# Two attention layers on one core: a score bank emptied and refilled by 256 columns instead of 512

## Chip, core and metric

The kernel is one program on one core of a Trainium2 chip. It is written in Python on a framework that gives each engine its own queue of instructions, worked off in order, and sets the semaphore waits from what the instructions read and write. The metric is the device time of one execution in microseconds (us), taken as the median of several runs. A profiled execution has its own time and a span, which runs from the start of its first to the end of its last instruction.

Five engines appear: PE (TensorE, matmuls; its weight loads are listed apart as PEld), DVE (VectorE), ACT (ScalarE), POOL (GpSimd) and SP (SyncE, which issues DMAs).

## The reference

Four blocks, each an attention-like layer and a feed-forward layer, are added to x of shape 4 x 1024 x 128 (batch, tokens, features), all in float32. The change touches only the two softmax attentions, in blocks L2 and L3. Both get layer-normed x, and `run` adds their output to x.

```python
# L2: 8 heads of 16
scores = einsum('bhsd,bhtd->bhst', q, k) / sqrt(16)
p = softmax(scores, axis=-1)
att = einsum('bhst,bhtd->bhsd', p, v)
out = att.reshape(S, B, D, H).sum(axis=-1).reshape(B, S, D)

# L3: 16 heads of 8, keys in blocks of 64, over which this is scanned
scores = einsum('bhqd,bhkd->bhqk', Q, K_blk) / sqrt(8)
m_new = maximum(m, scores.max(-1, keepdims=True))
corr, exp_scores = exp(m - m_new), exp(scores - m_new)
chunk_sum = exp_scores.sum(-1, keepdims=True)
l = chunk_sum * corr + chunk_sum            # not l * corr
out = out * corr + einsum('bhqk,bhkd->bhqd', exp_scores, V_blk)
# after the last block: out / l, then out @ out_w.T + out_b
```

## The kernel before

**Layout.** `attention` serves both layers. Heads go in groups of four. Head j of a group lies on partitions 32j to 32j+31, so that four matmuls of 32 rows can run beside each other in four row strips of TensorE. L2 has 8 groups (4 batches, 2 each) and L3 has 16. Queries and keys are kept transposed (features on partitions, 1024 tokens along the row). One further row holds minus the row maximum in q and ones in k, so a score comes out with its maximum already subtracted. The values have a column of ones, which makes the sums of the softmax come out beside the output.

**Turns and rounds.** A group is worked on twice, 16 turns each time. First it is *scanned*: query blocks of 128 against 512 keys at a time, only to find the row maxima. Then it is *weighed*: 128 keys (`kc`) against 512 queries (`n`) at a time, exponentials taken and multiplied with the values. While group m is weighed, group m + 1 is scanned. A turn has two rounds. A round, in the order of the code of the loop at the end of `attention`, is:

1. `weigh` of a first head: one matmul of 128 x 512 into a PSUM bank `pb` (line 1319), then its exponential by ACT into `es` (line 1323).
2. `score` of two heads of the other group into a two-bank tile `pa` (line 1265), and a maximum over it by DVE (line 1273 or 1277).
3. `weigh` of a second head, with another bank `pb` and another exponential.
4. `gather` (line 1341): the exponentials of an earlier turn times the values of four heads, 256 query columns, into the bank `po`.
5. Jobs that belong to this turn and round, such as projections, `negate` (maxima into q by way of DRAM) and `collect`.

In round 0 of a turn the weighed heads are 2 and 3 and the scored ones 0 and 1; in round 1 it is the other way round. So each round's four matmuls lie in four different row strips. A float32 matmul appears in the profile as two passes, each with a weight load of its own. `gather` is skipped in the round that would take the first half of a `kc` of 0, and takes all 512 columns one round later.

**Counts.** There are (8 + 16) x 16 x 2 = 768 weighing rounds, 24 x 16 x 4 = 1536 exponentials, and 3072 passes at line 1319. In the first 16 turns of a layer nothing is weighed (`scan_alone`), and in the last 16 nothing is scanned.

**Banks.** PSUM has eight banks of 512 float32 per partition. Here `pa` takes four (two tiles of two), `po` one, and a pool called `sm` has three, which rotate: each `weigh` takes the next. Call a round's first head A and its second head B. With two banks taken per round and three in rotation, B of a round takes the bank that A of the round before has left, and A takes the bank that B of two rounds before has left. An engine's queue is in order: when the weight load of B waits for its bank, the `gather` behind it waits too.

**Elsewhere, for comparison.** Block L0 has other PSUM tiles that the prediction reads. `wide` (line 324) is four banks: one use writes the columns 0 to 255 of each bank (inputs `bt`, `kt`), and ACT copies them to `kk` (line 348); the other use writes columns 256 to 511 (inputs `qp`, `kt`), and DVE multiplies them with a mask into `mt` (line 413). `tp` is one bank of two halves, which ACT copies one after the other into `kt` (line 339) and `bt` (line 341). Line 486 has four matmul passes of 256 columns behind each other.

Of the kernel before, what the change touches and what calls it, by code (L numbers as in the profile page):

```python
# [9 lines left out]
F32 = mybir.dt.float32  # L10
AF = mybir.ActivationFunctionType
ALU = mybir.AluOpType
AX = mybir.AxisListType
PSUM = bass.MemoryType.PSUM

P = 128
# [11 lines left out]
class Net:  # L28
# [1087 lines left out]
    def attention(self, H, HD, scale, weights, prepare, finish, last=False):  # L1116
# [13 lines left out]
        nc, tc = self.nc, self.tc  # L1130
# [3 lines left out]
        TURNS = 2 * TPB  # L1134
        NBM = 9 if last else 2
        wq, wk, wv = weights
        with ExitStack() as c:
# [1 line left out]
            two = c.enter_context(tc.tile_pool(name="at2", bufs=2))  # L1139
            dram = c.enter_context(tc.tile_pool(name="atd", bufs=1, space=bass.MemoryType.DRAM))  # L1140
            pap = c.enter_context(tc.tile_pool(name="ata", bufs=2, space=PSUM))
            sm = c.enter_context(tc.tile_pool(name="ats", bufs=3, space=PSUM))
            pop = c.enter_context(tc.tile_pool(name="ato", bufs=1, space=PSUM))
            qcol, kcol, vrow = prepare(one, sm)
            md = dram.tile([M, 2, 4, 4, P], F32, tag="md", name="md")
            ones = one.tile([1, 4, 32], F32, tag="ones1", name="ones1")
            nc.gpsimd.memset(ones, 0.0)
            nc.gpsimd.memset(ones[:, :, HD : HD + 1], 1.0)
            cp = sm.tile([P, 1], F32, tag="sm", name="cp")
            nc.tensor.matmul(  # L1150
                cp, lhsT=ones.rearrange("p a b -> p (a b)"), rhs=self.ones[0:1, 0:1], start=True, stop=True
            )
            col = one.tile([P, 1], F32, tag="onec", name="onec")
            nc.vector.tensor_copy(col, cp)
            kring = [one.tile([P, SEQ], F32, tag=f"k{i}", name=f"k{i}") for i in range(3)]
            qring = [one.tile([P, SEQ], F32, tag=f"q{i}", name=f"q{i}") for i in range(3)]
            zero = one.tile([4, 256], F32, tag="zero", name="zero")
# [123 lines left out]
            def scan_alone(m, turn):  # L1281


                st = state[m]
                i, n = turn // 2, turn % 2
                if n == 0:
                    both = [scan(m, turn, hp) for hp in range(2)]
                    for j in range(4):
                        both[j // 2][0](j)
                    for _, reduce in both:  # L1290
                        reduce()
                    return
                banks = [sm.tile([P, 512], F32, tag="sm", name="pb") for _ in range(3)]
                banks.append(pop.tile([P, 512], F32, tag="po", name="pb"))
                for j in range(4):
                    r = slice(32 * j, 32 * j + 32)
                    nc.tensor.matmul(
                        banks[j], lhsT=st["q"][r, i * P : (i + 1) * P],
                        rhs=st["k"][r, n * 512 : (n + 1) * 512], start=True, stop=True,
                    )  # L1300
                for j in range(4):
                    out = st["bm"][i // 4][:, i % 4, j, :]
                    if last:
                        nc.vector.tensor_reduce(  # L1304
                            out[:, 1:9], banks[j].rearrange("p (c s) -> p c s", c=8), axis=AX.X, op=ALU.max
                        )
                    else:
                        nc.vector.tensor_reduce(out[:, n : n + 1], banks[j], axis=AX.X, op=ALU.max)  # L1308

            def weigh(m, turn, j):  # L1310

                st = state[m]
                n, kc = turn // TPB, turn % TPB
                es = st.setdefault("es", {})
                if turn not in es:
                    es[turn] = two.tile([P, 4, 512], F32, tag="es", name="es", bufs=5)
                pb = sm.tile([P, 512], F32, tag="sm", name="pb")
                r = slice(32 * j, 32 * j + 32)
                nc.tensor.matmul(  # L1319
                    pb, lhsT=st["k"][r, kc * P : (kc + 1) * P], rhs=st["q"][r, n * 512 : (n + 1) * 512],  # L1320
                    start=True, stop=True,
                )
                nc.scalar.activation(es[turn][:, j, :], pb, AF.Exp, scale=scale)  # L1323

            def gather(m, turn, half):

# [44 lines left out]
            for b in range(NB):  # L1371

                t = b * G * TURNS
# [5 lines left out]
            for m in range(M):  # L1379
                t = m * TURNS  # L1380
# [15 lines left out]
            t = 0  # L1396
            while t < (M + 1) * TURNS or jobs:
                scans, weighs = TURNS <= t < M * TURNS, TURNS <= t < (M + 1) * TURNS
                if t < TURNS:
                    scan_alone(0, t)  # L1400
                for rnd in range(2):

                    other = 2 - 2 * rnd
                    if scans:
                        score, reduce = scan(t // TURNS, t % TURNS, rnd)
                    if weighs:
                        weigh(t // TURNS - 1, t % TURNS, other)
                    if scans:
                        for j in range(2):
                            score(2 * rnd + j)  # L1410
                        reduce()
                    if weighs:
                        weigh(t // TURNS - 1, t % TURNS, other + 1)

                    w, half = (t - 2, 1) if rnd == 0 else (t - 1, 0)
                    if TURNS <= w < (M + 1) * TURNS:
                        gather(w // TURNS - 1, w % TURNS, half)
                    for what, args in jobs.pop((t, rnd), ()):
                        what(*args)
                t += 1  # L1420
# [10 lines left out]
    def l2_attn(self):  # L1431
        nc, a = self.nc, self.a2
        H, HD = 8, 16
        self.layernorm(twice=(a["gamma"], a["beta"]))
        with self.tc.tile_pool(name="a2", bufs=1) as one:

            wv = one.tile([P, P], F32, tag="wvs", name="wvs")
            nc.vector.tensor_reduce(wv, a["wv"].rearrange("p (d j) -> p d j", j=8), axis=AX.X, op=ALU.add)

            def prepare(pool, psum):  # L1440
                row = pool.tile([1, P], F32, tag="row", name="row")
                nc.vector.tensor_reduce(row, a["bv"].rearrange("p (d j) -> p d j", j=8), axis=AX.X, op=ALU.add)
                vp = psum.tile([P, P], F32, tag="sm", name="vp")
                nc.tensor.matmul(vp, lhsT=self.ones[0:1, :], rhs=row, start=True, stop=True)
                vrow = pool.tile([P, P], F32, tag="vrow", name="vrow")
                nc.vector.tensor_copy(vrow, vp)
                return a["bq"], a["bk"], vrow

            def finish(b, o, sums, corr, pool, pair):

                rec = pool.tile([P, 8, H], F32, tag="rec", name="rec")

                def weights():
                    tp = pair("tp").rearrange("p (r h) -> p r h", r=8)
                    sv = sums.rearrange("p (s r) -> p r s", r=8)
                    for r in range(8):
                        nc.tensor.transpose(tp[:, r, 0:H], sv[:, r, :], self.ident[0:H, 0:H])
                    nc.vector.reciprocal(rec, tp[:, :, 0:H])

                def turn():  # L1460
                    tp = pair("tp2").rearrange("p (r h d) -> p r h d", r=8, h=H)
                    ov = o.rearrange("p (s r) -> p r s", r=8)
                    for r in range(8):
                        nc.tensor.transpose(tp[:, r, :, :].rearrange("p h d -> p (h d)"), ov[:, r, :], self.ident)
                    ob = pool.tile([P, H, 8, HD], F32, tag="ob", name="ob")
                    nc.vector.tensor_mul(
                        ob.rearrange("p h r d -> p r h d"), tp, rec.unsqueeze(3).to_broadcast([P, 8, H, HD])
                    )
                    xs = self.x[:, b * TPB : (b + 1) * TPB, :]
                    nc.gpsimd.tensor_add(xs, xs, ob.rearrange("p h r d -> p h (r d)"))  # L1470

                return [weights, turn]

            self.attention(H, HD, 0.25, (a["wq"], a["wk"], wv), prepare, finish)

    def l2_ffn_load(self):
# [349 lines left out]
```

## Time and profile before

| what | value |
|---|---|
| median of 3 runs | 2668.34 us (2666.43 to 2669.78) |
| the profiled execution | 2665.29 us |
| its span, first to last instruction | 2663.6 us |
| PE busy | 2417.5 us, 91% of the span |
| DVE, ACT, POOL busy | 1795.2, 1501.7, 293.0 us |
| stretch with weighing in L2 (1012 to 1480 us) | 468 us: PE 467.6, ACT 284.2 busy |
| stretch with weighing in L3 (1607 to 2530 us) | 923 us: PE 921.7, ACT 574.0 busy |
| granted TensorE clock in both stretches | 1.00 |

The time of the profiled execution is 1.7 us above its span and 3.05 us below the median of the runs. The busy times count an engine as busy when any of its instructions runs. Four matmuls in four row strips are one busy stretch of PE, also when three of the strips have ended and the fourth is late.

### The profile page before, as it was taken

How to read it: one execution, taken by the hardware profiler on the slowest of the kernel's cores; microseconds unless marked ns; L12 is line 12 of the kernel's file. 1: busy time of each engine (PE TensorE's matmuls, PEld its weight loads, DVE VectorE, ACT ScalarE, POOL GpSimd, SP SyncE). 2: the span in 40 equal slices, each digit the busy share in tenths (PEclk: the TensorE clock that was granted, in tenths of full speed). 3: DMA queues.
4: the chain of work that ended last, by engine and by line, in shares of the span. 5: the costliest groups of instructions: out<-in, count | busy, mean ns of one | idle time of the engine just before them, and what ended most of it. 6: DMA issues, size and time to landing. Idle time of an engine off the chain costs nothing.

```text
span 2663.6 us, 51041 instructions
## 1 busy us (share of the span) xinstructions
PE 2417.5 (91%) x19913; PEld 1222.1 (46%) x19913; DVE 1795.2 (67%) x3670; ACT 1501.7 (56%) x3333; POOL 293.0 (11%) x525
## 2 busy tenths in 40 slices
PE   5687758899997979999999779999999999999968
PEld 3455535699995333333333443333333333333356
DVE  5888877476764767776774357767767776777233
ACT  4466468455554434665566635666666566666632
POOL 6012021000002530000000440000000000000011
PEclk8699879899997989999999879999999999999969
DMA  1333320000000001001000000000000000000000
GB/s 45 74 77 74 73 74 1 1 1 1 1 1 2 1 9 18 14 15 18 14 14 6 5 5 10 9 10 8 8 9 12 8 9 10 8 8 8 3 18 18
DMA packets 116719, 46.66 MB, mean 18 GB/s; under 512 B 88473, under 2 KB 111097, under 8 KB 116474
## 3 DMA queue, kind: packets, MB, share of 16 engines
q1 hardware_dynamic: 116474, 43.35, 8.2%
q8 instruction: 159, 2.61, 0.4%
q14 instruction: 86, 0.70, 0.1%
HBM read 17.04 MB, written 12.98 MB: 11 GB/s over the span
## 4 chain that ended last, share of the span: by engine, by line
PE 57%; DVE 4%; ACT 1%; POOL 1%; issue 1%; SPq 0%; DMA 0%; POOLq 0%; DVEq 0%; ACTq 0%
PE pb L1319 32%; PE po L1341 16%; PE pa L1265 2%; DVE bm L1277 1%; PE pp L1205 1%; PE pv L1186 1%; DVE bm L1304 1%; PE tp L158 1%; PE gp L1014 1%; PE rp L1743 1%; DVE bm L1308 0%; PE pr L1598 0%; PE rp L1520 0%; PE ph L1756 0%; POOL sg L1753 0%
## 5 line engine op out<-in xcount | busy, mean ns | idle before, releaser
L1323 ACT ACTIVATE es<-pb 128x512 f32<-128x512 f32 x1536 | 836.3, 594 | 536.1 <-PE pb L1319 381.8
L1319 PE MATMUL pb<-q,k 32*128 32x512 f32 x3072 | 956.5, 641 | 3.9 <-DVE bm L1308 1.7
L1265 PE MATMUL pa<-k,q 32*128 32x512 f32 x2944 | 846.0, 650 | 10.4 <-DMA q<-q 10.3
L1277 DVE TENSOR_REDUCE bm<-pa 128x2 f32<-128x1024 f32 x496 | 605.0, 1225 | 261.1 <-PE pb L1319 168.0
L1341 PE MATMUL po<-es,v 128*32 128x256 f32 (+1 forms) x5760 | 480.0, 405 | 0.0
L1319 PEld LDWEIGHTS pb<-q,k 32*128 32x128 f32 x3072 | 313.5, 183 | 350.7 <-ACT es L1323 189.8
L1341 PEld LDWEIGHTS po<-es,v 128*32 128x32 f32 x5760 | 114.2, 108 | 543.1 <-issue 508.2
L1273 DVE TENSOR_REDUCE bm<-pa 128x16 f32<-128x1024 f32 x240 | 293.2, 1222 | 97.3 <-PE pb L1319 60.7
L1265 PEld LDWEIGHTS pa<-k,q 32*128 32x128 f32 x2944 | 234.4, 186 | 37.0 <-issue 18.6
L152 POOL TENSOR_SCALAR xn<-x,rs,nm 128x128 f32<-128x128 f32 x112 | 50.3, 464 | 1204.6 <-DVE nm L125 1026.9
L366 DVE TENSOR_TENSOR pr<-T,L 128x31 f32<-128x31 f32 (+15 forms) x248 | 92.0, 371 | 28.0 <-DMA L<-ld 20.7
L369 DVE TENSOR_TENSOR T<-T,pr 128x31 f32<-128x31 f32 (+15 forms) x248 | 93.1, 375 | 8.5
L1348 DVE COPY oT<-po 128x512 f32<-128x512 f32 x48 | 32.8, 682 | 95.6 <-PE po L1341 95.6
L158 PE MATMUL tp<-ident,xn 128*128 128x128 f32 x224 | 47.0, 361 | 42.7 <-ACT xn L154 38.1
L821 ACT ACTIVATE w<-tr,half 128x128 f32<-128x128 f32 x128 | 47.1, 368 | 48.3 <-PE tr L819 45.6
L796 ACT ACTIVATE a<-hp,wb 128x128 f32<-128x128 f32 x128 | 47.1, 368 | 41.6 <-PE hp L792 40.1
L1081 PE MATMUL ep<-L_ffn_expert_w,xnT 128*128 128x512 f32 x128 | 66.8, 654 | 3.3 <-DVE x L1090 3.1
L324 PE MATMUL wide<-bt,kt 32*128 32x128 f32 x512 | 29.9, 360 | 43.9 <-DVE mt L413 31.7
L486 PE MATMUL sp<-ux,kn 128*128 128x256 f32 x128 | 46.1, 493 | 17.7 <-ACT ux L475 17.7
L158 PEld LDWEIGHTS tp<-ident,xn 128*128 128x128 f32 x224 | 33.9, 179 | 61.2 <-ACT xn L154 47.0
L804 DVE TENSOR_TENSOR dlt<-gr,mask 128x128 f32<-128x128 f32 x96 | 28.0, 292 | 48.3 <-PE gr L802 48.3
L853 ACT COPY dr<-tr 128x128 f32<-128x128 f32 x128 | 34.1, 266 | 43.1 <-PE tr L851 41.1
(466 smaller groups left out, 3598.8 us busy)
## 6 DMA issues: line engine op xcount, KB each, us to landing
ld<-kk SPq DMA_DIRECT2D x128, 32.0 KB
L<-ld SPq DMA_DIRECT2D x8, 512.0 KB
td<-T SPq DMA_DIRECT2D x8, 512.0 KB
tb<-td SPq DMA_DIRECT2D x128, 32.0 KB
md<-nt SPq DMA_DIRECT2D x192, 2.0 KB
q<-md SPq DMA_DIRECT2D x192, 2.0 KB
x<-in_L_attn_x_dram SPq DMA_DIRECT2D x4, 512.0 KB
od<-o SPq DMA_DIRECT2D x32, 64.0 KB
```

The source lines that it names most:

```text
L152: nc.gpsimd.tensor_scalar(xn[:, i, :], src[:, i, :], sl, bl, ALU.mult, ALU.add)
L158: nc.tensor.transpose(tp[:, i, :], xn[:, 4 * n + i, :], self.ident)
L366: nc.vector.tensor_mul(pv, T[:, 0 : j + 1, j : j + 1].to_broadcast(sh), L[:, j : j + 1, j + 1 :].to_broadcast(sh))
L369: nc.vector.tensor_sub(T[:, 0 : j + 1, j + 1 :], T[:, 0 : j + 1, j + 1 :], pv)
L796: nc.scalar.activation(self.a, self.hp, AF.Silu, bias=B1)
L1081: nc.tensor.matmul(ep.rearrange("p a b -> p (a b)"), lhsT=self.tok(t), rhs=ew[:, 4 * h : 4 * h + 4, :].rearrange("p a b -> p (a b)"), star ...
L1265: nc.tensor.matmul(pa[:, j % 2, :], lhsT=st["q"][r, i * P : (i + 1) * P], rhs=st["k"][r, n * 512 : (n + 1) * 512], start=True, stop=True,)
L1273: nc.vector.tensor_reduce(out[:, :, 1:9], pa.rearrange("p j (c s) -> p j c s", c=8), axis=AX.X, op=ALU.max)
L1277: nc.vector.tensor_reduce(out[:, :, n : n + 1], pa, axis=AX.X, op=ALU.max)
L1319: nc.tensor.matmul(pb, lhsT=st["k"][r, kc * P : (kc + 1) * P], rhs=st["q"][r, n * 512 : (n + 1) * 512], start=True, stop=True,)
L1323: nc.scalar.activation(es[turn][:, j, :], pb, AF.Exp, scale=scale)
L1341: nc.tensor.matmul(po[r, cols], lhsT=vring[b % 2][:, kc, 4 * g + j, :], rhs=es[:, j, cols], start=kc == 0, stop=True, skip_group_check=True,)
```

## The change

- The pool `sm` gets one buffer per tag, and three tiles `eb` with the tags sm0, sm1 and sm2 are made once. `weigh` takes them in turn, by a counter, where it took the pool's next tile before. `scan_alone` uses the same three. So the rotation of banks stays as it was.
- The first head of a round (`early`) is still one matmul over 512 columns, but its exponential is taken by two ACT instructions of 256 columns each.
- The second head is two matmuls of 256 columns each into its bank, and its exponential is one ACT instruction of 512 columns as before.
- Two small tiles, `cp` and `vp`, which are used once before the rounds, get a tag of the new pool.

```diff
-            sm = c.enter_context(tc.tile_pool(name="ats", bufs=3, space=PSUM))
+            sm = c.enter_context(tc.tile_pool(name="ats", bufs=1, space=PSUM))
...
+            eb = [sm.tile([P, 512], F32, tag=f"sm{i}", name=f"eb{i}") for i in range(3)]
...
-                banks = [sm.tile([P, 512], F32, tag="sm", name="pb") for _ in range(3)]
+                banks = list(eb)
...
-            def weigh(m, turn, j):
+            turned = [0]
+
+            def weigh(m, turn, j, early):
...
-                pb = sm.tile([P, 512], F32, tag="sm", name="pb")
+                pb = eb[turned[0] % 3]
+                turned[0] += 1
                 r = slice(32 * j, 32 * j + 32)
-                nc.tensor.matmul(
-                    pb, lhsT=st["k"][r, kc * P : (kc + 1) * P], rhs=st["q"][r, n * 512 : (n + 1) * 512],
-                    start=True, stop=True,
-                )
-                nc.scalar.activation(es[turn][:, j, :], pb, AF.Exp, scale=scale)
+                whole, halves = (slice(0, 512),), (slice(0, 256), slice(256, 512))
+                for cols in whole if early else halves:
+                    nc.tensor.matmul(
+                        pb[:, cols], lhsT=st["k"][r, kc * P : (kc + 1) * P],
+                        rhs=st["q"][r, n * 512 + cols.start : n * 512 + cols.stop], start=True, stop=True,
+                    )
+                for cols in halves if early else whole:
+                    nc.scalar.activation(es[turn][:, j, cols], pb[:, cols], AF.Exp, scale=scale)
...
-                        weigh(t // TURNS - 1, t % TURNS, other)
+                        weigh(t // TURNS - 1, t % TURNS, other, True)
...
-                        weigh(t // TURNS - 1, t % TURNS, other + 1)
+                        weigh(t // TURNS - 1, t % TURNS, other + 1, False)
```

More of the change, by code (lines that the diff above doesn't have):

```diff
@@ L1148, in attention @@
             nc.gpsimd.memset(ones[:, :, HD : HD + 1], 1.0)
-            cp = sm.tile([P, 1], F32, tag="sm", name="cp")
+            cp = sm.tile([P, 1], F32, tag="sm1", name="cp")
             nc.tensor.matmul(
@@ L1442, in prepare @@
                 nc.vector.tensor_reduce(row, a["bv"].rearrange("p (d j) -> p d j", j=8), axis=AX.X, op=ALU.add)
-                vp = psum.tile([P, P], F32, tag="sm", name="vp")
+                vp = psum.tile([P, P], F32, tag="sm0", name="vp")
                 nc.tensor.matmul(vp, lhsT=self.ones[0:1, :], rhs=row, start=True, stop=True)
```

## The prediction

> **What bounds the kernel now.** I first read the page's chain of work that ended last, to see which engine and line the time hangs on in the two weighing stretches:
>
> ```profile
> PE 57%; DVE 4%; ACT 1%; POOL 1%; issue 1%; SPq 0%; DMA 0%; POOLq 0%; DVEq 0%; ACTq 0%
> PE pb L1319 32%; PE po L1341 16%; PE pa L1265 2%; DVE bm L1277 1%; PE pp L1205 1%; PE pv L1186 1%; DVE bm L1304 1%; PE tp L158 1%; PE gp L1014 1%; PE rp L1743 1%; DVE bm L1308 0%; PE pr L1598 0%; PE rp L1520 0%; PE ph L1756 0%; POOL sg L1753 0%
> ```
>
> PE alone carries the chain, and half the span lies on the weighing matmuls and the gather. PE is busy 1389.3 of the 1391.0 us of the four windows that make up these stretches. That hides something: PE counts as busy while one of four row strips is late. So the second view is the timeline of the weight loads in two rounds, where each load's start shows when its strip was let go:
>
> ```profile
> 1257.50 0.16 PEld L1341 LDWEIGHTS po<-es,v 128*32 128x32 f32 x8 [0.76 <-issue]
> 1258.07 0.18 PEld L1319 LDWEIGHTS pb<-q,k 32*128 32x128 f32 x1 [0.41 <-issue]
> 1258.08 0.19 PEld L1265 LDWEIGHTS pa<-k,q 32*128 32x128 f32 x2
> ...
> 1258.24 0.29 PEld L1319 LDWEIGHTS pb<-q,k 32*128 32x128 f32 x2
> 1259.29 0.16 PEld L1341 LDWEIGHTS po<-es,v 128*32 128x32 f32 x8 [0.76 <-issue]
> 1259.86 0.18 PEld L1319 LDWEIGHTS pb<-q,k 32*128 32x128 f32 x1 [0.41 <-ACT es L1323]
> ...
> 1259.88 0.27 PEld L1319 LDWEIGHTS pb<-q,k 32*128 32x128 f32 x2
> ...
> 1260.93 0.16 PEld L1341 LDWEIGHTS po<-es,v 128*32 128x32 f32 x8 [0.76 <-issue]
> ```
>
> A is loaded at 1258.07 and B at 1258.24, 0.17 later; in the next round (1259.86) B follows at 1259.88, after 0.02. The gather, queued behind B, starts 1.22 after A in the first and 1.07 in the second. The round from 1258.07 lasts 1.79, the one before it (A at 1256.43 in the same timeline) 1.64. What lets B go is in ACT's timeline:
>
> ```profile
> 1257.59 1.08 ACT L1323 ACTIVATE es<-pb 128x512 f32<-128x512 f32 x2 [1.45 <-PE pb L1319]
> 1259.23 1.08 ACT L1323 ACTIVATE es<-pb 128x512 f32<-128x512 f32 x2 [0.56 <-PE pa L1265]
> ```
>
> An exponential takes 0.60 (0.594 is the page's mean); the two overlap by about 0.1. A's of the round from 1256.43 starts at 1257.59, 1.16 after A, and ends at 1258.19; B's load starts 0.05 later into that bank. So B may start X = 1.16 + 0.60 + 0.05 = 1.81 after A of the round before. A round that B does not delay lasts T = 1.64. After such a round B is late by 1.81 - 1.64 - 0.02 = 0.15, that round lasts 1.79, and after it B is late by 1.81 - 1.79 - 0.02 = 0. **So rounds go in pairs, and a pair lasts T + X - 0.02 = 3.43 us.** Every load of line 1319 read so: in 361 of 768 rounds B is within 0.04 of A, in 319 it is 0.14 to 0.20 behind, in 85 more than 0.20 (rounds after one without a gather, or in which ACT stood behind the corrections of `negate`). The 384 pairs make 1317 of the two stretches' 1391 us; the rest are jobs.
>
> Thus ACT, idle 0.56 before the pair of exponentials shown, matters by one thing: when A's bank is free.
>
> **The change, part by part.** *Does B start when the first half is out?* That is the step all else hangs on. Trace of before has one place where a matmul goes into columns of a bank of which other columns are being read, the tile `wide`:
>
> ```profile
> 198.03 1.22 DVE L413 TENSOR_TENSOR mt<-wide,upper 128x1024 f32<-128x1024 f32 x1
> ...
> 198.21 0.37 ACT L339 COPY kt<-tp 128x256 f32<-128x256 f32 x1
> ...
> 198.48 0.38 ACT L341 COPY bt<-tp 128x256 f32<-128x256 f32 x1
> ...
> 199.39 0.73 PE L324 MATMUL wide<-bt,kt 32*128 32x128 f32 x16 [0.86 <-DVE mt L413]
> ```
>
> The matmuls of `bt`, `kt` write columns 0 to 255, DVE reads 256 to 511. The matmuls' inputs are there at 198.86, but they start at 199.39, and DVE, done at 199.25, is named as releaser. Nothing but the shared bank ties them. In the whole trace PE waits 12 times, 31.7 us, for `mt` there, and none of the 1024 matmuls overlaps one of the 64 reads of `wide`. So the program orders accesses by the bank, not by columns, and I take it that B's first half waits for *both* halves of A's exponential: the change would then not do what it says.
>
> The Trainium skill has a rule on it ("PSUM — Partial Sum Buffer", section "PSUM bank collisions raise a hardware error"): guard PSUM by bank and quadrant, not by address, since two engines in one bank and quadrant at once collide even at disjoint columns. All four quadrants are touched here by both sides. The rule goes further than the row, which shows a wait and not what an overlap would do. By the rule no legal program gains the early start and the time is the forecast below; without it the first rival's.
>
> *A's exponential in halves.* What ACT needs for two 256-column reads of one bank, against one of 512:
>
> ```profile
> 205.42 0.37 ACT L339 COPY kt<-tp 128x256 f32<-128x256 f32 x1
> 205.69 0.38 ACT L341 COPY bt<-tp 128x256 f32<-128x256 f32 x1
> ...
> 209.51 0.59 ACT L388 COPY qp<-pq 128x512 f32<-128x512 f32 x1
> ```
>
> The two end at 206.07, 0.65 after the first began; the one takes 0.59. So X grows by 0.06. These are copies; an exponential of 512 at 0.594 is within 0.01 of the copy, so I take 0.06. Below: by spacing alone a half adds 0.27 (205.42 to 205.69) and a whole 0.49, so 0.05; nearly nothing, 0.02, if exponentials hide their fixed part better. Above: the 128x256 activation at line 1752 takes 0.418, 0.04 more than the copy; twice that on top is 0.14. Below zero only if halves release the bank separately, which is the first rival. The 768 extra ACT instructions are otherwise hidden in ACT's idle time (0.06 of 0.56 a round); if that cover went, each would cost the same 0.06.
>
> *B in two matmuls.* Four passes of 256 with four loads replace two of 512 with two loads, 1536 more of each in all. No row strip runs passes of 256 in before; the nearest are four passes of 256 of the whole array, beside B's two passes now:
>
> ```profile
> 169.77 1.13 PE L486 MATMUL sp<-ux,kn 128*128 128x256 f32 x4
> ```
>
> B now runs from 1258.24 to 1259.37 (its second pass starts at 1258.78 and takes 0.59), also 1.13. So T grows by 0 to 0.01; I take 0.005. The extra loads are hidden behind the passes before them, of some 0.21 each. If that cover fails, it is the third rival.
>
> The skill speaks against this here ("TensorE: Matmul & The Clock Gate", section "Part 3: Packing small matmuls — row/col tiling"): a weight load overlaps running matmuls only when its row group differs, and the page gives a load as columns / 1.2, so an estimated 107 ns for 128. By it two more loads stand bare in each round, T is 1.85, X no longer binds, a pair is 3.70, and the sum would be 384 x 0.27 = 104 us. The row of four passes disagrees, and the row decides.
>
> *The wait.* B's first load waits at the head of PE's queue as B's load did. Behind it stand the gather's eight loads, and behind them the next round's A, so ACT and DVE are late with it. B's second matmul finds its bank free.
>
> *At nothing:* the counter and tags issue no instruction; banks rotate as before, also in `scan_alone`; A's matmul is the same; B's exponential is one instruction, as before. DVE's maxima, 1.22 of a round, have a free tile of two to run into.
>
> *Sum.* A pair becomes 1.645 + 1.87 - 0.02 = 3.495, 0.065 more. 384 x 0.065 = 25 us on the profiled execution's 2665.3 us (span 2663.6 and 1.7 around it), so 2690. The median of the runs shown is 3.0 above that execution, so I state **2693 us**. Bounds: 384 x 0.02 = 8 and 384 x (0.14 + 0.01) = 58, so 2676 to 2726. The 85 late rounds pay up to the whole 0.06 and not half of it: at most 85 x 0.03 = 2.6 us more, inside the bounds.
>
> **The rivals.**
>
> *Faster: the bank is really left by halves.* If B's first matmul starts 0.05 after A's *first* half, X = 1.16 + 0.38 + 0.05 = 1.59, under T + 0.02, so B is never late in ordinary rounds. The second half is free 0.27 later, while B's first two passes of the four need about half of 1.13. A pair is 2 x 1.645 = 3.29, 0.14 less: 384 x 0.14 = 54 us, 2614. It decides from the point where X falls under 1.66. For it: the halves are written for that. Against it: every row of `wide`.
>
> *No change.* ACT's two halves take no longer than the whole, and the halves release together. The sum is 384 x 0.005 = 2 us, 2670. Against it: the 0.06 of the copies.
>
> *Much slower: B's loads bare.* In the round at 1258.07 A's second load starts 0.11 after its first (the row at 1258.18 in that timeline). If two more such loads stood before B's passes in every round, T = 1.86, X no longer binds, a pair is 3.72, 0.29 more: 111 us, 2779. Against it: the four passes of line 486 in 1.13.
>
> **How the numbers follow.** Forecast (both halves awaited, ACT's cost as bounded) 0.80; the faster rival 0.11, as PE waiting for ACT on half a bank is seen once only (1.2 us) and DVE's case is the main witness; no change 0.06; bare loads 0.03. A measurement of this kernel can tell about 0.2%, 5 us, from no change. So: faster 0.11, the same 0.06, slower 0.80 + 0.03 = 0.83. The forecast's bounds, with the no-change case at their lower end, hold 0.86; the range is 2670 to 2726.
>
> **What would show it.** In the new profile: 768 exponentials of 512 columns and 1536 of 256; a pair of halves of about 0.65 to 0.66; B's first load 0.05 after the end of the *second* half; B late by some 0.21 in every second round; pairs of 3.49. The forecast is wrong if B's load starts while the second half is read, if the pair of halves takes over 0.74 or under 0.61, or if four passes of B take longer than 1.15.

## The result and the profile after

The changed kernel takes 2695.29 us in the median of 4 runs (2693.9 to 2709.6), the kernel before 2669.06 us (4 runs, 2666.43 to 2674.61). By the medians it is 26.2 us slower, where 25 were forecast. The ratio of the runs is 1.0113, with a 95% interval of 1.0089 to 1.0137, or some 30 us, as one of the four runs lies at 2709.6. Executions far above the others of their kernel (one of e1 at 3524.8 us, one of e4 at 3018.0, and four of e9's 11 at 2720 to 2724, its profiled one among them) count in the medians of the table below, but not in its ratios. The profiled execution took 2693.9 us with a span of 2692.2, 28.6 more than before. From the first to the last exponential of each layer it spends 474.9 and 937.5 us where before took 465.9 and 921.3: 25.2 us of the 28.6 lie there. The other 3.4 lie outside of these stretches. There the profiles of other kernels below differ from before as much and more, whatever their edit (e1 by +2.6, e2 by -5.9, e3 by +11.6), so I do not put the 3.4 down to the change.

The page's chain of work has the same shape as before (`eb` is the old `pb`, line 1326 the old 1319, line 1349 the old 1341):

```profile
PE 57%; DVE 3%; ACT 1%; POOL 1%; issue 1%; SPq 0%; DMA 0%; POOLq 0%; DVEq 0%; ACTq 0%
PE eb L1326 31%; PE po L1349 16%; PE pa L1266 4%; PE pp L1206 1%; DVE bm L1278 1%; PE pv L1187 1%; DVE bm L1305 1%; PE tp L158 1%; PE gp L1014 1%; PE rp L1751 1%; DVE bm L1309 0%; PE pr L1606 0%; PE rp L1528 0%; PE ph L1764 0%; PE kp L1519 0%
```

By this view little has changed but the span: a strip that waits beside busy strips is not seen in it. The timeline of the weight loads of two rounds shows it, as it did before:

```profile
1264.75 0.16 PEld L1349 LDWEIGHTS po<-es,v 128*32 128x32 f32 x8 [0.33 <-issue]
1265.32 0.18 PEld L1326 LDWEIGHTS eb<-q,k 32*128 32x128 f32 x1 [0.41 <-issue]
...
1265.54 0.72 PEld L1326 LDWEIGHTS eb<-q,k 32*128 32x128 f32 x4
1266.59 0.16 PEld L1349 LDWEIGHTS po<-es,v 128*32 128x32 f32 x8 [0.33 <-issue]
1267.16 0.18 PEld L1326 LDWEIGHTS eb<-q,k 32*128 32x128 f32 x1 [0.41 <-ACT es L1331]
...
1267.18 0.27 PEld L1326 LDWEIGHTS eb<-q,k 32*128 32x128 f32 x2
...
1268.24 0.16 PEld L1349 LDWEIGHTS po<-es,v 128*32 128x32 f32 x8 [0.33 <-issue]
```

B follows A by 0.22 in the first round (1265.32, 1265.54) and by 0.02 in the second. The rounds last 1.84 and 1.65, from A at 1265.32 over 1267.16 to the next work at 1268.81: a pair of 3.49, where 3.495 was predicted and 3.43 measured before. What released B at 1265.54 is in ACT's timeline of the round that began at 1263.67:

```profile
1264.83 1.15 ACT L1331 ACTIVATE es<-eb 128x256 f32<-128x256 f32 x3 [1.45 <-PE eb L1326]
1266.47 1.15 ACT L1331 ACTIVATE es<-eb 128x256 f32<-128x256 f32 x3 [0.50 <-PE pa L1266]
```

A row stands for three instructions, A's two halves and B's whole. One by one in the trace, A's halves end 0.384 and 0.658 after the start of the first, so at 1265.21 and 1265.49. B's load comes 0.05 after the second and 0.33 after the first. So it is throughout: 316 of 768 rounds have B 0.18 to 0.24 late (319 were 0.14 to 0.20 late before), and B's distance to the end of the second half is 0.05 in nearly every one of them. The trace also has the semaphore marks of each instruction: of A's two halves the first raises no semaphore in 766 of 768 rounds, and the second raises the one that B's load waits for. So B waits by the program, which gives it nothing that tells of the first half alone. The four passes of B, in PE's timeline, take as long as its two did:

```profile
1265.54 0.90 PE L1326 MATMUL eb<-q,k 32*128 32x256 f32 x2
...
1266.08 0.59 PE L1326 MATMUL eb<-q,k 32*128 32x256 f32 x2
```

From 1265.54 to 1266.67 is 1.13, as from 1258.24 to 1259.37 before.

### The profile page after: what moved, and what is told of

Same layout as the page of the kernel before. It is cut to its first block, busy times and chain, and to the rows that moved or that the text cites. A ratio compares the mean times of both kernels' runs of the same rounds, so it can differ in the third digit from the quotient of the medians.

```text
span 2692.2 us, 54885 instructions
## 1 busy us (share of the span) xinstructions
PE 2448.0 (91%) x21449; PEld 1521.3 (57%) x21449; DVE 1796.3 (67%) x3670; ACT 1548.5 (58%) x4101; POOL 291.7 (11%) x525
## 4 chain that ended last, share of the span: by engine, by line
PE 57%; DVE 3%; ACT 1%; POOL 1%; issue 1%; SPq 0%; DMA 0%; POOLq 0%; DVEq 0%; ACTq 0%
PE eb L1326 31%; PE po L1349 16%; PE pa L1266 4%; PE pp L1206 1%; DVE bm L1278 1%; PE pv L1187 1%; DVE bm L1305 1%; PE tp L158 1%; PE gp L1014 1%; PE rp L1751 1%; DVE bm L1309 0%; PE pr L1606 0%; PE rp L1528 0%; PE ph L1764 0%; PE kp L1519 0%
## 5 line engine op out<-in xcount | busy, mean ns | idle before, releaser
L1331 ACT ACTIVATE es<-eb 128x256 f32<-128x256 f32 (+1 forms) x2304 | 884.1, 455 | 514.6 <-PE eb L1326 374.9
L1326 PE MATMUL eb<-q,k 32*128 32x256 f32 (+1 forms) x4608 | 981.6, 481 | 4.1 <-DVE bm L1309 1.7
L1326 PEld LDWEIGHTS eb<-q,k 32*128 32x128 f32 x4608 | 606.2, 184 | 388.0 <-ACT es L1331 178.0
L1266 PEld LDWEIGHTS pa<-k,q 32*128 32x128 f32 x2944 | 241.6, 187 | 30.7 <-DVE bm L1278 16.3
```

The lines of the kernel that those rows point to most:

```text
L1266: nc.tensor.matmul(pa[:, j % 2, :], lhsT=st["q"][r, i * P : (i + 1) * P], rhs=st["k"][r, n * 512 : (n + 1) * 512], start=True, stop=True,)
L1326: nc.tensor.matmul(pb[:, cols], lhsT=st["k"][r, kc * P : (kc + 1) * P], rhs=st["q"][r, n * 512 + cols.start : n * 512 + cols.stop], start= ...
L1331: nc.scalar.activation(es[turn][:, j, cols], pb[:, cols], AF.Exp, scale=scale)
```

## The experiments

Three numbers are read from each trace. *Scanned rounds*: the time of the 704 rounds that weigh one group and scan another (both layers), from the start of A's exponential in the first to that in the round after the last. *Pair*: two ordinary rounds there, the median. *Last turns*: 30 rounds of the 16 turns in which nothing is scanned, for L2 and for L3. Each ratio is to runs of before made beside that kernel. The first and the last are sums over long stretches of one profiled execution, so they scatter far less than a whole execution.

| kernel | median, us | ratio to before (95%) | scanned rounds | pair | last turns |
|---|---|---|---|---|---|
| before | 2669.06 | | 1276.9 | 3.43 | 52.3, 52.3 |
| the change | 2695.29 | 1.0113 (1.0089 to 1.0137) | 1299.9 | 3.49 | 53.3, 53.3 |
| e1_fixed_banks | 2666.75 | 0.9998 (0.9988 to 1.0008) | 1276.9 | 3.43 | 52.3, 52.3 |
| e2_exp_halves | 2706.40 | 1.0149 (1.0134 to 1.0164) | 1297.7 | 3.49 | 53.2, 53.2 |
| e2_again | 2691.82 | 1.0090 (1.0065 to 1.0115) | 1297.8 | 3.49 | 53.2, 67.5 |
| e3_matmul_halves | 2668.30 | 1.0008 (0.9996 to 1.0019) | 1279.7 | 3.43 | 52.4, 52.4 |
| e4_other_exp_halves | 2671.18 | 1.0005 (0.9992 to 1.0017) | 1277.9 | 3.43 | 52.3, 52.3 |
| e5_exp_quarters | 2762.61 | 1.0359 (1.0341 to 1.0378) | 1339.9 | 3.62 | 68.9, 68.9 |
| e6_tail_banks | 2777.47 | 1.0396 (1.0377 to 1.0415) | 1277.7 | 3.43 | 103.0, 101.7 |
| e7_tail_own_tiles | 2655.04 | 0.9962 (0.9947 to 0.9977) | 1277.5 | 3.43 | 46.9, 46.9 |
| e8_half_exp_left_out | 2615.04 | 0.9792 (0.9771 to 0.9813) | 1226.8 | 3.28 | 49.8, 49.8 |
| e9_tail_half_banks | 2681.11 | 1.0028 (1.0010 to 1.0047) | 1278.1 | 3.43 | 67.1, 86.4 |
| e10_tail_halves_own_tiles | 2663.67 (one run) | | 1277.5 | 3.43 | 51.5, 51.0 |

### Which part costs

Four kernels take the change apart. Their edits against the changed kernel:

```diff
# e1_fixed_banks: neither is halved
-                for cols in whole if early else halves:
+                for cols in whole:
-                for cols in halves if early else whole:
+                for cols in whole:
# e2_exp_halves, e2_again: only A's exponential is halved
-                for cols in whole if early else halves:
+                for cols in whole:
# e3_matmul_halves: only B's matmul is halved
-                for cols in halves if early else whole:
+                for cols in whole:
# e4_other_exp_halves: B's exponential is halved, nothing else
-                for cols in whole if early else halves:
+                for cols in whole:
-                for cols in halves if early else whole:
+                for cols in whole if early else halves:
```

> The changed kernel with both edits of size taken back: only the three fixed banks remain, every matmul and every exponential of the weighing is over 512 columns. Theory (the loss is the longer hold of A's bank): no change from before, 2669 us within 2, pairs of rounds 3.43 us. Rival (the fixed banks set other waits than the rotating pool): most of the loss stays, some 2690 us and more.

> Fixed banks, and only the exponential of a round's first head A in two halves; B is one matmul of 512 columns again. Theory: the whole loss is here, 384 pairs x 0.06 = 23 us, about 2692 us; B is late by 0.21 us in every second round and pairs last 3.49 us. Rival (the four passes and loads of B are what costs): 2669 us.

> Fixed banks, and only B in two matmuls of 256 columns; A's exponential is one instruction again. Theory: 0 to 4 us slower than before (0.005 to 0.01 us in 384 pairs), 2669 to 2673 us. Rival (B's passes and loads are what costs): about 2695 us.

> Fixed banks, and the exponential of the second head B in two halves, A's whole: the same number of extra ACT instructions, on the bank that nobody is waiting for. Theory: ACT's idle 0.5 us of a round hides the 0.06, 2669 us within 2. Rival (each extra ACT instruction costs, wherever it stands): 384 x 0.06 to 768 x 0.06, so 2692 to 2715 us.

Measured, in scanned rounds against before: 0.0, +20.8, +2.8 and +1.0 us; the change itself has +23.0. The fixed banks cost nothing. The extra ACT instructions on B's bank cost nothing in ordinary rounds: e4's 1.0 arises in the first five rounds of L2 and does not grow in the 699 after them. A's exponential in halves has 20.8 of the 23.0, and B's matmuls 2.8: some 2.0 of it is 352 pairs x 0.0055, the rest arises in the first rounds of the layers. So the loss belongs to the one bank that someone waits for, and not to the number of instructions: e4 has as many exponentials as e2.

The whole time of e2 is above what its scanned rounds explain: +39 us in the median, while its profiled execution lay 14 us above the median of before. It was run again:

> The kernel with only A's exponential in halves, a second time: its timed runs lay at 2682 and 2688 and four times at 2706 to 2711 us, while its profiled execution (2682) spent 22.9 us more than before in the two weighing stretches. Theory: the weighing costs 23 us in every execution and the further 15 to 20 us are outside of it or a state of the chip, so that a new set of runs has its stretches at +23 and its median anywhere from 2688 to 2708. Rival (B whole behind a longer hold costs more than B in halves does): the stretches of a profile near 2706 are 35 to 40 us longer than before.

The median was 2692 this time, and the profiled execution fell on a long one, 2711.4 us. Its scanned rounds are those of the first profile within 0.1; 14.3 us more stand in L3's last turns. Busy time and clock of 28 us before and 28 us after the point where it begins there:

```profile
core 0: us, PE busy (x) PEld busy (x) DVE busy (x) ACT busy (x) POOL busy (x), PEclk, DMA share, GB/s
2510.00:2538.00 28.00, 27.84 (x184) 9.08 (x184) 4.71 (x27) 18.03 (x48) 0.00 (x0) 1.00 0.04 6
2540.00:2568.00 28.00, 28.00 (x116) 6.35 (x108) 0.00 (x0) 10.02 (x28) 0.00 (x0) 0.50 0.00 1
```

The granted clock (the column PEclk) is halved there. By its number the rival came true: the two stretches of this profile are 37.3 us longer than before. Its reason did not: B whole costs no more than B in halves, since the scanned rounds are the same in both profiles of e2 and 2 us shorter than the change's; the rest is the clock in one layer's last turns. 6 of e2's 12 timed executions lie above 2700 us; one of the changed kernel's four does (2709.6), which was not profiled. Each execution has its mean granted clock on record, and it fits: 0.920 to 0.924 in those six and 0.919 in the changed kernel's, against 0.926 to 0.931 in all the others of these kernels. Where in the changed kernel the clock fell is not shown.

### How the cost goes with the time that A's bank is held

e5 makes the hold longer and e8 shorter, both with B whole and against e1:

```diff
# e5_exp_quarters
+                quarters = [slice(128 * i, 128 * i + 128) for i in range(4)]
-                for cols in whole:
+                for cols in quarters if early else whole:
                     nc.scalar.activation(es[turn][:, j, cols], pb[:, cols], AF.Exp, scale=scale)
# e8_half_exp_left_out
+                if early:
+                    nc.gpsimd.memset(es[turn][:, j, 256:512], 1.0)
-                for cols in whole:
+                for cols in halves[:1] if early else whole:
                     nc.scalar.activation(es[turn][:, j, cols], pb[:, cols], AF.Exp, scale=scale)
```

> Fixed banks, B one matmul, and A's exponential in four instructions of 128 columns. Theory: X grows by what four reads of one bank take over one. From rows of before, copies of 128 columns behind each other end 0.155 us apart and one alone takes 0.27, so 3 x 0.155 + 0.27 = 0.73 against 0.59: 0.14, and 384 pairs x 0.14 = 54 us more than before, 2722 us; pairs of rounds 3.57 us. Rival (the loss comes from having a second instruction at all, or from the order of the banks, and not from the length of the hold): as with two halves, about 2692 us, pairs 3.49 us.

Scanned rounds: +63.0 us, an ordinary pair 3.615 against 3.428, so 0.187 more and not 0.14. ACT's timeline and that of the loads, from A's exponential to B's load of the next round:

```profile
1246.64 1.27 ACT L1332 ACTIVATE es<-eb 128x128 f32<-128x128 f32 x5 [0.70 <-PE eb L1326]
```

```profile
1247.12 0.18 PEld L1326 LDWEIGHTS eb<-q,k 32*128 32x128 f32 x1 [0.41 <-issue]
...
1247.47 0.29 PEld L1326 LDWEIGHTS eb<-q,k 32*128 32x128 f32 x2
```

B's load at 1247.47 is 0.35 behind A and 0.83 behind the start of the exponential: a hold of 0.785 in the trace and 0.05. I had expected 0.73, with ends 0.155 apart. That spacing, in the trace of before, is of a copy behind a longer activation and not of equal instructions; the four exponentials here end 0.169 apart (0.278 for the first, 0.785 for all). The hold was mis-sized, the law was not: the hold is 0.188 longer than the whole exponential's 0.597, a pair 0.187. The rival (a second instruction as such) is out. The other 33 us of this kernel are in the last turns, where its clock was at 0.5 for 34 us in each layer.

> Fixed banks, matmuls whole, and of A's exponential only the first 256 columns are computed; the other 256 are set to 1 by POOL, so half of A's softmax is left out. A's bank is free 0.21 us earlier than before, as it would have been for B's first half if the halves could be left one by one. Theory (the hold of A's bank alone makes every second round late): B is never late in ordinary rounds, pairs of rounds 3.28 us, the scanning and weighing rounds 52 us shorter than before (352 pairs x 0.147). Rival (something else is due as soon as the wait is gone, such as DVE's maxima or the gather): pairs stay over 3.36 us and less than half of that comes.

Half of A's softmax is missing here, so this is a measurement and no candidate. Scanned rounds are 50.1 us shorter, a pair is 3.28:

```profile
1228.61 0.18 PEld L1326 LDWEIGHTS eb<-q,k 32*128 32x128 f32 x1 [0.41 <-ACT es L1333]
1228.63 0.27 PEld L1326 LDWEIGHTS eb<-q,k 32*128 32x128 f32 x2
...
1229.68 0.16 PEld L1351 LDWEIGHTS po<-es,v 128*32 128x32 f32 x8 [0.76 <-issue]
1230.25 0.18 PEld L1326 LDWEIGHTS eb<-q,k 32*128 32x128 f32 x1 [0.41 <-ACT es L1333]
1230.27 0.27 PEld L1326 LDWEIGHTS eb<-q,k 32*128 32x128 f32 x2
```

B is 0.02 behind A in every ordinary round, and rounds last 1.64. So nothing else was due when the wait went. About this, by estimate, the change would have gained if the first half alone had released B; the kernel also spares ACT work and keeps B in one matmul, so it is not the same program. Put in a row, holds of 0.384, 0.597, 0.659 and 0.785 us give pairs of 3.28, 3.43, 3.49 and 3.62 (3.615): from 0.597 on a pair grows by what the hold grows.

### What holds a bank together: the tile

In the last turns the scan's four banks are free, so whole outputs can be kept while banks are added. The edit of e6 and, below it, of e7 (both against e1; the list `more` is appended to the ring of three banks in `weigh`):

```diff
# e6_tail_banks
+                if t == M * TURNS:
+                    free = pap.tile([P, 2, 512], F32, tag="pa", name="free")
+                    more = [free[:, 0, :], free[:, 1, :]]
# e7_tail_own_tiles
+                if t == M * TURNS:
+                    more = [pap.tile([P, 512], F32, tag="pa", name=f"free{i}") for i in range(2)]
```

> The fixed banks with whole matmuls and exponentials; in the last 16 turns of a layer, in which nothing is scanned, the rotation has five banks (two of the scan's). Theory: B never waits there, so 16 pairs in each layer drop from 3.42 to 3.26 us: 2 x 16 x 0.16 = 5 us, 2663 to 2664 us; the last 31 round starts of a layer span 49 to 50 us and not 54.1. Rival (the wait is hidden by something else, such as ACT or the gather): no change, 2668 us.

(The 54.1 there is for 31 rounds; for the 30 of the table it is 52.3.) It went the other way, to 2777 us. With the ring in this order, A and B of one round can lie in the two banks of `free`. Loads and exponentials of e6's first such round:

```profile
1430.15 0.29 PEld L1327 LDWEIGHTS free<-q,k 32*128 32x128 f32 x2 [0.41 <-issue]
1432.02 0.29 PEld L1327 LDWEIGHTS free<-q,k 32*128 32x128 f32 x2 [1.57 <-ACT es L1332]
```

```profile
1431.37 0.60 ACT L1332 ACTIVATE es<-free 128x512 f32<-128x512 f32 x1 [0.61 <-PE free L1327]
1433.18 0.60 ACT L1332 ACTIVATE es<-free 128x512 f32<-128x512 f32 x1 [1.21 <-PE free L1327]
```

B, in another bank than A, is loaded at 1432.02, 0.05 after the end of A's exponential at 1431.97. So the program's waits hold the whole tile, two banks of it too. Then the clock fell to 0.50 for nearly all of the last turns of both layers, which doubled the rest.

> As the run with five banks in the last 16 turns of a layer, but each of the two added banks is a tile by itself; there they were two banks of one tile, and B in the one waited until the exponential of A in the other had ended. Theory (waits are set by tile, and with tiles of their own B never waits): full rounds of 1.63 us one after another in the last 16 turns, the last 31 round starts of a layer span 47 to 49 us and not 52.3, 2663 us in all if TensorE keeps its full clock there. Rival (waits there come from something else than the shared tile): rounds of 3 us at half clock as in that run, some 2770 us.

With a tile for each bank the last turns take 46.9 us where they took 52.3, at full clock, and the kernel 0.9962 of before (0.9947 to 0.9977), some 10 us less: it beats both kernels, by 0.4% and more. Its median is 8 us below the 2663 that were expected; in the profiled execution 9.5 us less lie between the first and last exponentials of the layers and 7.5 outside of them, where the edit does nothing. Three gathers, with the loads between them:

```profile
1436.43 0.16 PEld L1350 LDWEIGHTS po<-es,v 128*32 128x32 f32 x8 [0.76 <-issue]
1436.99 0.30 PEld L1327 LDWEIGHTS eb<-q,k 32*128 32x128 f32 x4 [0.41 <-issue]
1438.05 0.16 PEld L1350 LDWEIGHTS po<-es,v 128*32 128x32 f32 x8 [0.76 <-issue]
...
1439.68 0.16 PEld L1350 LDWEIGHTS po<-es,v 128*32 128x32 f32 x8 [0.76 <-issue]
```

Gathers are 1.62 and 1.63 apart, and A's and B's loads go together. The two rounds without a gather, each with the one behind it, gain 1.57 us as well (3.85 to 2.28 in L3), so it is 5.4 us a layer and not the 2.5 of e6's expectation.

e9 and e10 put the two halves of every head of the last turns into two banks, 256 columns used of each, with two matmuls and two exponentials for each head and three such sets in turn:

```diff
# e9_tail_half_banks: two sets are tiles of two banks
+                    free = [pap.tile([P, 2, 512], F32, tag="pa", name=f"free{i}") for i in range(2)]
+                    sets = [(eb[0], eb[1])] + [(f[:, 0, :], f[:, 1, :]) for f in free]
# e10_tail_halves_own_tiles: two sets of two tiles; the third is one bank of one tile
+                    free = [pap.tile([P, 512], F32, tag="pa", name=f"free{i}") for i in range(2)]
+                    sets = [(eb[0], eb[1]), (eb[2], free[0]), (free[1][:, 0:256], free[1][:, 256:512])]
```

> As before in the rounds that scan. In the last 16 turns of a layer each head of a round takes two banks and uses 256 columns of each, in a rotation of three such sets, with two matmuls and two exponentials per head: the halves are left and filled in banks of their own, and B again takes the set that A of the round before leaves. Theory (a half is held by its bank alone): B's first load starts when the first half is out, no later than 0.05 us after it, is late in no ordinary round, and the last 31 round starts of a layer span 49 to 51 us, against 54.1 before and some 55 in the changed kernel. Rival (halves don't let B start earlier even in banks of their own, since matmuls wait for the head's whole exponential): 55 us.

By itself this run settles nothing: the last turns were longer, 67.1 and 86.4 us, but the clock was at 0.50 in 33 and 81 us of them, and two of the three sets were tiles of two banks, of which e6 shows that they are held whole.

> In the last 16 turns of a layer the two halves of a head lie in two banks, each a tile by itself, in two of three sets; the third set is one bank of one tile for both halves. Theory (a half can be left and filled by itself when it has a tile by itself): B's first load follows A's within 0.03 us where its set is of two tiles, and waits for the second half's exponential, some 0.2 us and more, where its set is the one tile. Rival (the halves of a head are held together whatever their tiles): B is late in the same way with all three sets.

B takes the set that A of the round before has left. Loads of two rounds of e10; in the first B's set is of two tiles (`eb`), in the second it is the one tile (`free`):

```profile
1436.29 0.18 PEld L1318 LDWEIGHTS free<-q,k 32*128 32x128 f32 x1 [0.41 <-ACT es L1323]
1436.30 0.18 PEld L1318 LDWEIGHTS eb<-q,k 32*128 32x128 f32 x1
...
1437.92 0.29 PEld L1318 LDWEIGHTS eb<-q,k 32*128 32x128 f32 x2 [0.41 <-issue]
1438.16 0.72 PEld L1318 LDWEIGHTS free<-q,k 32*128 32x128 f32 x6
```

The exponentials of the two A that left these sets:

```profile
1435.81 0.66 ACT L1323 ACTIVATE es<-eb 128x256 f32<-128x256 f32 x2
...
1437.45 0.66 ACT L1323 ACTIVATE es<-free 128x256 f32<-128x256 f32 x2 [0.70 <-PE eb L1318]
```

In the first round B is loaded at 1436.30, 0.01 behind A, while the second half of the set is still being read (until 1436.47; the first was out at 1436.20). In the second, the halves share a tile, and B waits from 1437.92 until 1438.16, which is 0.05 after both halves are out (1438.11) and 0.33 after the first (1437.83). That is the changed kernel's wait again. The semaphore marks agree: in the last turns of e10 each half with a tile of its own raises a semaphore, and of the halves that share a tile the first does not, in 42 of 43 heads. So the theory holds: halves can be left one by one, if each has a tile; the rival is out.

## Why the prediction was right

**The bound.** Pairs of T + X - 0.02 held: 3.43 before and 3.49 after, and in e5 the pair grew with the hold, 0.187 for 0.188.

**B waits for both halves.** Right in its outcome, in every round. Its *reason* was too narrow: I wrote that the program orders accesses by the bank, and the row of `wide` cannot tell bank from tile, as `wide` is one tile. e6 shows two banks of one tile held together, e10 halves in tiles of their own let go. Whether one bank used by two tiles would still be held was not tried. So the rule cited from "PSUM — Partial Sum Buffer" was neither needed nor tested.

**A's exponential in halves.** 0.06 was predicted for the hold, from two copies; it is 0.659 - 0.597 = 0.062. The Trainium skill gives a figure for it ("ScalarE: Activation LUTs", section "What ACT_TABLE_LOAD costs"): 186 ns per instruction with immediate operands, of which some 93 overlap with the one before, so an estimated 0.09 for one more. The trace's 0.06 decides.

**B in two matmuls.** 0.005 a pair was taken, 0.01 the bound; an ordinary pair of e3 has 0.0055. By the Trainium skill's rule ("TensorE: Matmul & The Clock Gate", section "Part 3: Packing small matmuls — row/col tiling"), by which a load overlaps only matmuls of another row group, it would have been an estimated 104 us. The scanned rounds of e3 have 2.8. The same section also lets a load into the background weight buffer run ahead, which the prediction left out; no run tells whether that is what happened here.

**The sum.** 25 us, and 25.2 in the two stretches. That the stated 2693 is within 3 us of the median is in part luck: the sum for the profiled execution was 2690 and it took 2693.9, with 3.4 us from outside of the stretches, while the median lies 1.4 above it and not the 3.0 that were added. **At nothing:** the fixed banks (e1, 0.0) are nothing, and ACT's extra work away from the wait is nothing in ordinary rounds (e4, +1.0 in all).

**What the prediction did not see:** that TensorE's clock can fall in the last turns, which cost 14 us in e2_again. It is in none of the rivals. Of the kernels with a longer hold the profiles show it in one of e2's four last turns, in both of e5's and in none of the changed kernel's. That the longer hold brings it on is not shown.

**The rivals.** The faster one (54 us from an early release) had about the right price, 56.0 in the two stretches of e8 (50.1 in the scanned rounds), and the wrong mechanism. Bare loads and no change are out.

## What to carry to other kernels

To split a read so that its buffer comes free by parts helps only if the parts are held apart; where the waits cover the whole tile, each part adds its fixed cost to the hold, here 0.06 us. Before pricing such a split, find a tile in the trace whose one part is written while the other is read, and see whether that ever overlaps. And read a concurrent engine strip by strip: PE was busy in 99.9% of these stretches, and over 100 us of late starts of B stood in them, of which e8 got 56 back.

## What the hardware showed that was not expected

In turns where only two of the four row strips and the gather run, the granted TensorE clock could drop to 0.50 and stay there, 34 us in e2_again with PE busy 28.00 of 28.00 us, and 99 and 95 us of 103 and 102 in e6. In e2_again it began behind a round without a gather (the lower clock is on record from 2539.9), and the same turns ran at 1.00 in before, the change and e7. What sets it off is open: e7 has the shortest rounds and kept its clock, so it is not the pace alone. One thing stands ahead of every such fall. In e2_again it is this stop of PE, 0.25 us with nothing running in any strip:

```profile
2536.63 1.62 PE L1326 MATMUL eb<-q,k 32*128 32x512 f32 x6
2538.50 1.12 PE L1326 MATMUL eb<-q,k 32*128 32x512 f32 x2 [0.25 <-ACT es L1331]
```

All eight falls in the last turns of e2_again, e5, e6 and e9 came 1.6 to 2.9 us after the beginning of a stop of PE of 0.18 to 1.5 us. In e7 and e8 PE has no such stop in the last turns, and the clock stayed. But stops of 0.18 to 0.25 us also stand in before, the change and e2's other last turns, and one of 0.51 in e10, with no fall behind them. So the stop is not enough by itself, and that it is the cause is not shown.
